# First product of the later slots of 256 rows in 7 products of half blocks, interleaved with the preceding slot's second product

## The chip, the cores and the metric

The kernel runs on one core of a Trainium2 chip. The metric is the device time of one execution in microseconds (us). The engines are PE (matrix products; PEld is its weight load), DVE, ACT and POOL (elementwise work) and SP (which issues most DMAs; "SPq" in a profile is its queue). DMAs move data between device memory and the on-chip memory (SBUF); products are accumulated in PSUM.

## What is computed

Two layers over 4096 tokens of width 256, all in float32. The second layer adds to each token a scan over time and the output of one of 8 experts, which is chosen by an argmax. This case is about the experts:

```
gate_logits = jnp.einsum('bsd,ed->bse', x, gate_w) + gate_b + expert_bias
top_idx = jnp.argmax(gate_logits, axis=-1)
for e in range(NUM_EXPERTS):                       # 8
    mask = (top_idx == e)[..., None].astype(x.dtype)
    h = jax.nn.relu(jnp.einsum('bsd,df->bsf', x, w1[e]) + b1[e])    # 256 -> 1024
    y = jnp.einsum('bsf,fd->bsd', h, w2[e]) + b2[e]                 # 1024 -> 256
    out = out + mask * y
```

The result is added to the token's row of the residual and the scan (the "base").

## The kernel before

The first layer and the scans come first (until about 900 us). By then the tokens lie in device memory sorted by expert (`xs_d`), each row with its token's number as a 257th column, and the base rows in `base_d`. Then come *slots*: 12 slots (`NF`) of 256 rows (`SL`, that is `SN` = 2 parts of 128), then slots of 128 rows, 8 (`MU`) always and further ones behind a test on the count `used`. A slot has one expert, read from `owner_i`; its rows begin at `at_i`.

For slot j:

- `weights(j)` (SP): four DMAs, w1 and w2 (1 MB each), b1 and b2, into tiles `w1p`, `w2p`, `b1p`, `b2p`. There are 3 of each for the slots of 256 rows and 3 others for those of 128.
- `slot_rows(j)` (SP): one DMA of the rows, from `xs_d` into `xrp` (4 tiles).
- `base_rows(j)` (POOL): an indirect DMA for each part, which gathers the base rows into `brp` (2 tiles) by the token numbers in `xrp`.
- `slot(j)` is a generator in five steps. Step 1: PE transposes the rows into `px` (L1104), and ACT (j < 2) or DVE copies them to `xTp` (L1106, L1108). Steps 2 and 3: the first product, 8 blocks f of 128 hidden units. For each, two matmuls (the two halves c of the 256 inputs) with 256 moving columns go to `ph` (L1114), and ACT (even f) or DVE (odd f) adds the bias, applies relu and writes `hT` (L1118, L1120); in slot 0 it is ACT alone. Step 4: the second product, for each of the two parts n 8 matmuls into `py` (L1127), and DVE adds the bias into `y` (L1130). Step 5: POOL adds the base rows (L1132) and scatters `y` to the output by indirect DMAs (L1134).

PE, SP, ACT and DVE run in the order in which the program is written; POOL's order in this stage is the scheduler's. The loop over the slots issues weights for slot j + 2 and rows for slot j + 2 at the start of slot j, then slot j's first product, the last step of slot j - 1, the transposes of slot j + 1, and slot j's second product. So on PE a slot is first product, transposes, second product. In slot 0, the transposes of slot 1 lie between the two products, and the last transposes of the scans (`pt`, L442), with the DVE adds (L445) and the write of `base_d` (L446) behind them, follow its second product.

The products of the first layer and the scan are already made of 7 products for 8 by `seven` (with Winograd's form of Strassen's scheme for 2x2 blocks); for the experts each block is multiplied as it is.

Of the kernel before, what the change touches and what calls it, by code (L numbers as in the profile page):

```python
# [47 lines left out]
PE, SP, ACT, DVE, POOL = (getattr(mybir.EngineType, k) for k in ("PE", "SP", "Activation", "DVE", "Pool"))  # L48
# [3 lines left out]
def tile_two_layers(  # L52
# [19 lines left out]
    nc = tc.nc  # L72
# [9 lines left out]
    ident = const.tile([P, P], F32, name="ident")  # L82
# [110 lines left out]
    psc1 = ctx.enter_context(tc.tile_pool(name="ps_scan", bufs=1, space=bass.MemoryType.PSUM))  # L193
# [231 lines left out]
    finished = []  # L425
# [47 lines left out]
    def rest_of(it):  # L473
        for _ in it:
            pass
# [9 lines left out]
    with ExitStack() as l0:  # L485
        wp = l0.enter_context(tc.tile_pool(name="w0", bufs=1, side="right"))
        wk = l0.enter_context(tc.tile_pool(name="work0", bufs=1, side="right"))
# [129 lines left out]
        def norm0(b, out):  # L617
            xn = wk.tile([P, NT, D], F32, name=f"xn_{b}", tag="xn")
            mv = small.tile([P, NT, 2], F32, name="mv")
            rstd = small.tile([P, NT], F32, name="rstd")  # L620
            out[b] = xnT = wk.tile([P, DC, TB], F32, name=f"xnT_{b}", tag="xnT", bufs=2)
            yield from layernorm(xs[b], xn, mv, rstd)
            yield
            if b == 0:

                fold()
                decay_mask()
                pt = [ps.tile([P, TB], F32, name=f"pt_{c}", tag=next(third)) for c in range(DC)]
# [12 lines left out]
            if b:  # L641
                cols0[b] = column_sums(wk, xnT, f"sums_{b}", 1)
            yield
# [249 lines left out]
        first = l0.enter_context(ExitStack())  # L893
# [4 lines left out]
        for b in range(NB):  # L898
            cols = cols0.pop(b)
            selb0 = selection(b, 0)  # L900
            back = norm1(b - 1) if b > 0 else iter(())
# [13 lines left out]
            if b + 1 < NB:  # L915
                ahead = norm0(b + 1, xnT)
# [25 lines left out]
        back = norm1(NB - 1)  # L942
# [24 lines left out]
    wk = ctx.enter_context(tc.tile_pool(name="work1", bufs=1, side="right"))  # L967
# [88 lines left out]
    sets = {}  # L1056
# [39 lines left out]
    def slot(j):  # L1096

        w1s, w2s, b1s, b2s = w1p(j), w2p(j), b1p(j), b2p(j)
        sn = parts(j)
        xr, xT, br = xrp(j), xTp(j)[:, :, : sn * P], brp(j)[:, :sn, :]  # L1100
        px = ps.tile([P, DC, sn * P], F32, name=f"px_{j}", tag="ps")
        for c in range(DC):
            for n in range(sn):
                nc.tensor.transpose(px[:, c, n * P : (n + 1) * P], xr[:, n, c * P : (c + 1) * P], ident)  # L1104
        if j < 2:
            nc.scalar.copy(xT, px)  # L1106
        else:
            nc.vector.tensor_copy(xT, px)  # L1108
        yield
        hT = wk.tile([P, FC, sn * P], F32, name=f"hT_{j}", tag="hT", bufs=2)  # L1110
        for f in range(FC):
            ph = ps.tile([P, sn * P], F32, name=f"ph_{j}_{f}", tag="ps")
            for c in range(DC):
                nc.tensor.matmul(  # L1114
                    ph, w1s[:, c, f * P : (f + 1) * P], xT[:, c, :], start=(c == 0), stop=(c == DC - 1)
                )
            if f % 2 == 0 or j == 0:
                nc.scalar.activation(hT[:, f, :], ph, AF.Relu, bias=b1s[:, f : f + 1])  # L1118
            else:
                nc.vector.tensor_scalar(hT[:, f, :], ph, b1s[:, f : f + 1], 0.0, ALU.add, ALU.max)  # L1120
            if f % (FC // 2) == FC // 2 - 1:
                yield
        y = wk.tile([P, sn, D], F32, name=f"y_{j}", tag="y", bufs=3)
        for n in range(sn):
            py = ps.tile([P, D], F32, name=f"py_{j}_{n}", tag="ps")
            for f in range(FC):
                nc.tensor.matmul(  # L1127
                    py, hT[:, f, n * P : (n + 1) * P], w2s[:, f, :], start=(f == 0), stop=(f == FC - 1)
                )
            nc.vector.tensor_add(y[:, n, :], py, b2s)  # L1130
        yield
        nc.gpsimd.tensor_add(y, y, br)  # L1132
        for n in range(sn):
            to = nc.gpsimd.indirect_dma_start(  # L1134
                out=out, out_offset=token(j, n), in_=y[:, n, :], in_offset=None, bounds_check=T - 1, oob_is_err=False
            )
            apart(to, written, "tokens' rows differ")
        yield


    scan_step(NB * UNITS - steps_done - 3 * CHUNKS + 1)
# [1 line left out]
    next(ends_filled)  # L1143
    scan_step(CHUNKS)
    rest_of(ends_filled)
    for j in range(3):
# [6 lines left out]
    cur, behind = slot(0), None  # L1153
    next(cur)
    used = nc.values_load(used_i[0:1, 0:1], min_val=MU, max_val=NU)

    taken = ExitStack()
    for j in range(NS):
        if j >= NF + MU:
            taken.enter_context(tc.If(used > j - NF))  # L1160
        if j + 2 < NS:
            weights(j + 2)
            if j > 0:
                slot_rows(j + 2)
        next(cur)
        next(cur)
        if behind:
            rest_of(behind)
        if j == 0:
            ahead = slot(j + 1)  # L1170
            next(ahead)
            next(cur)
            rest_of(finished.pop(0))
            base_rows(0)
# [4 lines left out]
            places(  # L1179
                tl, w1p=([P, DC, FF], 3), w2p=([P, FC, D], 3), b1p=([P, FC], 3), b2p=([P, D], 3),  # L1180
                xrp=([P, 1, D + 1], 4), xTp=([P, DC, P], 2), brp=([P, 1, D], 2),
            )
        if j + 1 < NS:
            base_rows(j + 1)
            if j > 0:
                ahead = slot(j + 1)
                next(ahead)
        if j > 0:
            next(cur)
        behind = cur  # L1190
        if j + 1 >= NF + MU:
            rest_of(behind)
            behind = None
        cur = ahead
    taken.close()


# [49 lines left out]
```

## Time and profile before

| | us |
|---|---|
| median of 3 runs | 1170.42 (1169.88 to 1173.16) |
| the profiled execution | 1170.57 |
| its span in the profile | 1168.8 |
| PE busy, share of the span | 1153.0, 99% |
| granted TensorE clock, mean | 0.998 |
| slots of 256 rows, first products start to slots of 128 rows | 902.27 to 1074.22 |
| slots of 128 rows, to the last second product's bias | 1074.22 to 1161.26 |

By stage, the busy times of the engines are:

| window, us | PE | PEld | DVE | ACT | POOL | DMA share |
|---|---|---|---|---|---|---|
| 931.9 to 1074.2 (slots 2 to 11) | 142.30 | 125.45 | 34.00 | 18.93 | 57.04 | 0.64 |
| 1074.2 to 1161.2 (slots of 128 rows) | 86.96 | 81.69 | 25.89 | 17.62 | 32.98 | 0.93 |

A line of the groups or of the timeline reads: line of the kernel, engine, operation, output<-inputs, shapes, count; then, in the groups, the busy time and the mean of one in ns, and the idle time before them with what ended it. In the timeline the first two columns are start and duration in us. In the chain of waits each line is a start, a duration and what ran then. A matmul of float32 stands as two instructions.

### The profile page before, as it was taken

The page shows a single profiled execution, that of the slowest core. Times are in us where ns is not written, and L with a number is a line of the kernel's source. Part 1 is how long each engine was busy: PE and PEld are TensorE (multiplying, and loading weights), DVE is VectorE, ACT ScalarE, POOL GpSimd, SP SyncE. Part 2 cuts the span into 40 slices and gives each one's busy share as a digit, 9 for nine tenths or more (in the row PEclk, how much of TensorE's full clock was granted, in tenths as well). Part 3 has the DMA queues.
Part 4 walks back from the last instruction along what each step waited for, and adds up shares of the span by engine and source line. Part 5 has one row for each costly group of instructions (what it writes and reads, how often), then busy time and mean ns, then how long its engine had stood idle before and what let it go on. Part 6 is the DMA issues. An engine that isn't in the chain of part 4 may idle for free.

```text
span 1168.8 us, 17270 instructions
## 1 busy us (share of the span) xinstructions
PE 1153.0 (99%) x6234; PEld 975.2 (83%) x6234; DVE 712.2 (61%) x1512; ACT 363.3 (31%) x719; POOL 314.6 (27%) x378
## 2 busy tenths in 40 slices
PE   8999999999999999999999999999999999999997
PEld 6887888888888888888888888888644888888996
DVE  5545736697579657876775797578799322222222
ACT  3112142444343333433343344343434111111221
POOL 6182220231014020402130231011053253333333
PEclk9999999999999999999999999999999999999999
DMA  8696563475256435535654465244258676683997
GB/s 255 214 352 236 156 218 144 141 240 186 99 185 212 146 139 167 201 135 178 223 192 135 148 203 186 100 167 154 90 155 250 246 236 214 212 300 134 332 367 265
DMA packets 89865, 231.33 MB, mean 198 GB/s; under 512 B 13885, under 2 KB 42705, under 8 KB 83121
## 3 DMA queue, kind: packets, MB, share of 16 engines
q1 hardware_dynamic: 81552, 202.77, 51.2%
q0 software_dynamic: 7792, 26.91, 6.3%
q8 instruction: 50, 0.82, 0.3%
q10 hardware_dynamic: 432, 0.52, 0.1%
q14 instruction: 39, 0.31, 0.1%
HBM read 206.75 MB, written 27.09 MB: 200 GB/s over the span
## 4 chain that ended last, share of the span: by engine, by line
PE 89%; DVE 5%; issue 2%; DMA 1%; POOL 1%; SPq 1%; ACT 0%; POOLq 0%; DVEq 0%
PE acc L765 21%; PE px_s L229 12%; PE px L229 10%; PE ph L1114 10%; PE py L1127 9%; PE pv_s L229 6%; PE pv L229 5%; PE py_s L229 3%; PE py L229 2%; PE px_yg L229 2%; PE pv L665 2%; PE po L711 1%; PE pv_yg L229 1%; PE pt L173 1%; DVE z L346 1%
## 5 line engine op out<-in xcount | busy, mean ns | idle before, releaser
L765 PE MATMUL acc<-vals,rs 128*128 128x256 f32 x1024 | 242.2, 380 | 0.0
L765 PEld LDWEIGHTS acc<-vals,rs 128*128 128x128 f32 x1024 | 194.2, 190 | 27.3 <-issue 1.4
L1114 PE MATMUL ph<-xTp,w1p 128*128 128x256 f32 (+1 forms) x768 | 129.8, 327 | 0.9 <-ACT xTp L1106 0.9
L1127 PE MATMUL py<-w2p,hT 128*128 128x256 f32 x576 | 128.3, 379 | 0.0
L1114 PEld LDWEIGHTS ph<-xTp,w1p 128*128 128x128 f32 x768 | 117.7, 191 | 11.4 <-ACT xTp L1106 1.1
L1127 PEld LDWEIGHTS py<-w2p,hT 128*128 128x128 f32 x576 | 107.7, 190 | 13.5
L348 POOL COPY last<-z 128x1 f32<-128x1 f32 x56 | 19.6, 352 | 340.6 <-DVE z L346 340.6
L1118 ACT ACTIVATE hT<-ph,b1p 128x256 f32<-128x256 f32 (+1 forms) x100 | 42.2, 422 | 212.4 <-PE ph L1114 157.6
L306 ACT ACTIVATE z<-z,bs 128x256 f32<-128x256 f32 (+1 forms) x156 | 87.4, 611 | 1.8 <-DVE z L255 1.8
L1120 DVE TENSOR_SCALAR hT<-ph,b1p 128x128 f32<-128x128 f32 (+1 forms) x92 | 38.1, 414 | 79.5 <-PE ph L1114 74.1
L229 PE MATMUL px_s<-sums,ws 128*128 128x256 f32 x312 | 81.3, 383 | 0.0
L1130 DVE TENSOR_TENSOR y<-py,b2p 128x256 f32<-128x256 f32 x36 | 15.3, 424 | 106.9 <-PE py L1127 94.9
L229 PE MATMUL px_s<-xn1T,ws 128*128 128x256 f32 x312 | 80.1, 379 | 0.0
L229 PE MATMUL pv_s<-sums,ws 128*128 128x256 f32 x312 | 80.1, 379 | 0.0
L346 DVE TENSOR_TENSOR_SCAN z<-z,last,z 128x512 f32<-128x512 f32 x56 | 75.7, 1351 | 0.0
L743 DVE SCALAR_TENSOR_TENSOR rs<-rs,selb 128x512 f32<-128x512 f32 x64 | 69.4, 1084 | 1.1
L229 PE MATMUL px<-xnT,keys 128*128 128x256 f32 x256 | 69.2, 393 | 0.1
L229 PE MATMUL px<-sums,keys 128*128 128x256 f32 x256 | 66.6, 383 | 0.0
L229 PE MATMUL pv<-sums,keys 128*128 128x256 f32 x256 | 66.5, 382 | 0.0
L229 PEld LDWEIGHTS px_s<-xn1T,ws 128*128 128x128 f32 x312 | 59.3, 190 | 8.1 <-issue 0.2
L229 PEld LDWEIGHTS pv_s<-sums,ws 128*128 128x128 f32 x312 | 59.3, 190 | 8.0
L229 PEld LDWEIGHTS px_s<-sums,ws 128*128 128x128 f32 x312 | 57.3, 190 | 9.9 <-ACT u_s L245 3.3
(236 smaller groups left out, 1842.3 us busy)
## 6 DMA issues: line engine op xcount, KB each, us to landing
ws<-wsum_d SPq DMA_DIRECT2D x39, 896.0 KB, 4.7
selb<-sel_d SPq DMA_DIRECT2D x64, 512.0 KB, 6.3
w1p<-in_w_dram SPq DMA_DIRECT2D x26, 1024.0 KB, 7.5
w2p<-in_w_dram SPq DMA_DIRECT2D x26, 1024.0 KB, 7.5
keys<-ksum_d SPq DMA_DIRECT2D x28, 896.0 KB, 8.6
vals<-in_e_vals_dram SPq DMA_DIRECT2D x32, 512.0 KB, 4.7
cb<-comb_d SPq DMA_DIRECT2D x32, 256.0 KB, 8.7
wsum_d<-wst POOLq DMA_DIRECT2D x6, 896.0 KB, 8.9
```

The costliest lines, as they stand in the source:

```text
L229: nc.tensor.matmul(to[:, q, :], w[:, q, at, :], cols[k - 1], start=start and q == 0, stop=True, skip_group_check=True,)
L306: nc.scalar.activation(z[ec][:, q, lo:hi], src[:, q, :], AF.Tanh if i == 1 else AF.Sigmoid, bias=bs[:, i, m, ec : ec + 1])
L346: nc.vector.tensor_tensor_scan(h, a[ec][:, m % 2, :], h, 0.0 if b == 0 else state, ALU.mult, ALU.add)
L348: nc.gpsimd.tensor_copy(state, h[:, TB - 1 : TB])
L665: nc.tensor.matmul(pv[-1][:, n % 2, :], xnT[:, c, n * P : (n + 1) * P], wv[:, c, :], start=(c == 0), stop=(c == DC - 1),)
L743: nc.vector.scalar_tensor_tensor(r[i][:, :, lo:hi], src, 0.0, selb[i][:, :, lo:hi], ALU.max, ALU.mult)
L765: nc.tensor.matmul(acc[n // 2][:, n % 2, :], lhsT, rhs, start=first and n % 2 == 0, stop=stop, skip_group_check=True)
L1114: nc.tensor.matmul(ph, w1s[:, c, f * P : (f + 1) * P], xT[:, c, :], start=(c == 0), stop=(c == DC - 1))
L1118: nc.scalar.activation(hT[:, f, :], ph, AF.Relu, bias=b1s[:, f : f + 1])
L1120: nc.vector.tensor_scalar(hT[:, f, :], ph, b1s[:, f : f + 1], 0.0, ALU.add, ALU.max)
L1127: nc.tensor.matmul(py, hT[:, f, n * P : (n + 1) * P], w2s[:, f, :], start=(f == 0), stop=(f == FC - 1))
L1130: nc.vector.tensor_add(y[:, n, :], py, b2s)
```

## The change

The slots of 256 rows are written as separate steps, and these are interleaved. While slot j's second product runs, the first product of slot j + 1 is made beside it: four times, a part of the first product and then a quarter of the second product (4 matmuls). After the second quarter come the transposes of slot j + 2. Slot 0's first product runs alone, and the transposes of slot 1 follow it.

For slots 4 to 11 (`PLAIN` = 4) the first product is made in 7 products (`first_sums7`). The blocks are: inner, the two halves c of the 256 inputs; rows of the result, hidden blocks of even and odd number (i); columns, the two parts k of 128 rows. One product is 4 matmuls (q) of 128 columns; three PSUM banks (`px`, `py`, `pv`) collect the products. The sums of weight blocks (4 of 128x512) are made by POOL one slot ahead, one of them in place in `w1p` (`first_weights`). The sums of row blocks (4 of 128x128) are made by DVE. DVE adds the bias and combines the banks (7 operations of 128x512), and ACT applies relu in place (4 of 128x512). The first products of slots 1 to 3, and of the slots of 128 rows, stay as they were.

The six tiles of each weight kind serve in turn (`in_turn`), for all slots, and weights are loaded three slots ahead. Rows of the slots of 256 are loaded for slots 0 to 3 ahead of all and then, behind slot j's scatter in the program, for slot j + 3. POOL's order in the slots is now the written one: in slot j the gathers of slot j + 1, the weight sums of slot j + 2, and slot j's last step. The slots of 128 rows keep their order of first product, transposes and second product.

```diff
-    w1p, w2p, b1p, b2p, xrp, xTp, brp = (placed(k) for k in ("w1p", "w2p", "b1p", "b2p", "xrp", "xTp", "brp"))
+    def in_turn(name):
+        return lambda j: [t for kind in sets[name] for t in kind][j % 6]
+    xrp, xTp, brp = (placed(k) for k in ("xrp", "xTp", "brp"))
+    w1p, w2p, b1p, b2p = (in_turn(k) for k in ("w1p", "w2p", "b1p", "b2p"))
...
+    PLAIN = 4
+    FP = FC // 2
+    wsums = {}
+    def quarters1(j):
+        w = w1p(j).rearrange("p c (q i h) -> p c q i h", q=FP, i=2)
+        return [w[:, c, :, i, :] for i in range(2) for c in range(DC)]
+    def first_weights(j):
+        a11, a12, a21, a22 = quarters1(j)
+        wsums[j] = tl.tile([P, 3, FP, P], F32, name=f"wsum1_{j}", tag="wsum1", bufs=2)
+        s4, s2, s3 = (wsums[j][:, k] for k in range(3))
+        nc.gpsimd.tensor_sub(s3, a11, a21)
+        nc.gpsimd.tensor_add(a21, a21, a22)
+        nc.gpsimd.tensor_sub(s2, a21, a11)
+        nc.gpsimd.tensor_sub(s4, a12, s2)
+    def first_sums7(j):
...
+        nc.vector.tensor_sub(t[:, 0, :], b12, b11)
+        nc.vector.tensor_sub(t[:, 1, :], b22, t[:, 0, :])
+        nc.vector.tensor_sub(t[:, 2, :], b22, b12)
+        nc.vector.tensor_sub(t[:, 3, :], b21, t[:, 1, :])
+        terms = {
+            1: (a11, b11), 2: (a12, b21), 3: (s4, b22), 4: (a22, t[:, 3, :]), 5: (s1, t[:, 0, :]),
+            6: (s2, t[:, 1, :]), 7: (s3, t[:, 2, :]),
+        }
+        def product(k, to, start):
+            w, x = terms[k]
+            for q in range(FP):
+                nc.tensor.matmul(
+                    to[:, q, :], w[:, q, :], x, start=start and q == 0, stop=True, skip_group_check=True
+                )
...
+        def biased(k, i, src):
+            u = tl.tile([P, FP, P], F32, name=f"ub{k}_{j}", tag=f"ub{k}")
+            nc.vector.tensor_tensor(u, src, bias[:, i].broadcast_to([P, FP, P]), ALU.add)
+            return u
+        def relu(i, k):
+            nc.scalar.activation(h[:, :, i, k, :], h[:, :, i, k, :], AF.Relu)
+        product(1, px, True)
+        product(2, py, True)
+        u1 = biased(1, 0, px)
+        nc.vector.tensor_add(h[:, :, 0, 0, :], py, u1)
+        relu(0, 0)
+        yield
+        product(6, px, False)
+        pv = psc1.tile([P, FP, P], F32, name=f"pv1_{j}", tag="pv")
+        product(7, pv, True)
+        u2 = biased(2, 1, px)
+        yield
+        product(5, px, False)
+        u4 = biased(4, 1, px)
+        nc.vector.tensor_add(h[:, :, 1, 1, :], pv, u4)
+        relu(1, 1)
+        yield
+        product(3, px, False)
+        product(4, pv, False)
+        nc.vector.tensor_add(h[:, :, 1, 0, :], pv, u2)
+        relu(1, 0)
+        nc.vector.tensor_tensor(h[:, :, 0, 1, :], px, bias[:, 0].broadcast_to([P, FP, P]), ALU.add)
+        relu(0, 1)
+        yield
...
+    ctx.enter_context(tc.manual_schedule(engines={POOL}))
+    rows(0)
     used = nc.values_load(used_i[0:1, 0:1], min_val=MU, max_val=NU)
+    rest_of(first(0, 4))
+    rows(1)
+    for j in range(NF):
+        weights(j + 3 if j else 2)
+        if j > 0:
+            base_rows(j + 1)
+            if PLAIN <= j + 2 < NF:
+                first_weights(j + 2)
+        if j + 1 < PLAIN:
+            ahead = first(j + 1, 4)
+        elif j + 1 < NF:
+            ahead = first_sums7(j + 1)
+        else:
+            ahead = first(j + 1, 2)
+        back = second(j)
+        for k in range(4):
+            next(ahead, None)
+            next(back)
+            if j == 0 and k == 0:
+                rest_of(finished.pop(0))
+                base_rows(0)
+                base_rows(1)
+            if k == 1:
+                rows(j + 2)
         if j == 0:
             table_only.close()
             scan_only.close()
...
+            weights(3)
+        finish(j)
+        if j > 0:
+            slot_rows(j + 3)
```

`rows`, `first`, `second` and `finish` are the old steps 1, 2 and 3, 4 and 5, with `second` giving way after each 4 matmuls.

More of the change, by code (lines that the diff above doesn't have):

```diff
@@ L1094, in base_rows, with rows @@
             nc.gpsimd.indirect_dma_start(out=brp(j)[:, n, :], out_offset=None, in_=base_d, in_offset=token(j, n))
-    def slot(j):
-        w1s, w2s, b1s, b2s = w1p(j), w2p(j), b1p(j), b2p(j)
+    hT, y = {}, {}
+    def rows(j):
         sn = parts(j)
-        xr, xT, br = xrp(j), xTp(j)[:, :, : sn * P], brp(j)[:, :sn, :]
+        xT = xTp(j)[:, :, : sn * P]
         px = ps.tile([P, DC, sn * P], F32, name=f"px_{j}", tag="ps")
@@ L1103, in slot @@
             for n in range(sn):
[L1104 removed]
+                nc.tensor.transpose(px[:, c, n * P : (n + 1) * P], xrp(j)[:, n, c * P : (c + 1) * P], ident)
         if j < 2:
@@ L1108, in slot, with hidden, first @@
             nc.vector.tensor_copy(xT, px)
-        yield
-        hT = wk.tile([P, FC, sn * P], F32, name=f"hT_{j}", tag="hT", bufs=2)
+    def hidden(j):
+        hT[j] = wk.tile([P, FC, parts(j) * P], F32, name=f"hT_{j}", tag="hT", bufs=2)
+        return hT[j]
+    def first(j, steps):
+        w1s, b1s = w1p(j), b1p(j)
+        sn = parts(j)
+        h = hidden(j)
         for f in range(FC):
@@ L1114, in slot @@
                 nc.tensor.matmul(
-                    ph, w1s[:, c, f * P : (f + 1) * P], xT[:, c, :], start=(c == 0), stop=(c == DC - 1)
+                    ph, w1s[:, c, f * P : (f + 1) * P], xTp(j)[:, c, : sn * P], start=(c == 0), stop=(c == DC - 1)
                 )
             if f % 2 == 0 or j == 0:
-                nc.scalar.activation(hT[:, f, :], ph, AF.Relu, bias=b1s[:, f : f + 1])
+                nc.scalar.activation(h[:, f, :], ph, AF.Relu, bias=b1s[:, f : f + 1])
             else:
-                nc.vector.tensor_scalar(hT[:, f, :], ph, b1s[:, f : f + 1], 0.0, ALU.add, ALU.max)
@@ L1121, in slot @@
-            if f % (FC // 2) == FC // 2 - 1:
+                nc.vector.tensor_scalar(h[:, f, :], ph, b1s[:, f : f + 1], 0.0, ALU.add, ALU.max)
+            if (f + 1) % (FC // steps) == 0:
                 yield
-        y = wk.tile([P, sn, D], F32, name=f"y_{j}", tag="y", bufs=3)
+    PLAIN = 4
[12 more added lines that the diff above has]
+        nc.gpsimd.tensor_sub(s4, a12, s2)
@@ new lines, in first_sums7 @@
+    def first_sums7(j):
+        a11, a12, s1, a22 = quarters1(j)
+        s4, s2, s3 = (wsums[j][:, k] for k in range(3))
+        b11, b12, b21, b22 = (xTp(j)[:, c, h * P : (h + 1) * P] for c in range(DC) for h in range(SN))
+        t = tl.tile([P, 4, P], F32, name=f"tsum1_{j}", tag="tsum1", bufs=2)
+        nc.vector.tensor_sub(t[:, 0, :], b12, b11)
[12 more added lines that the diff above has]
+                )
+        h = hidden(j).rearrange("p (q i) (k t) -> p q i k t", i=2, k=SN)
+        bias = b1p(j).rearrange("p (q i) -> p i q", i=2).unsqueeze(3)
+        def biased(k, i, src):
[4 more added lines that the diff above has]
+            nc.scalar.activation(h[:, :, i, k, :], h[:, :, i, k, :], AF.Relu)
+        px, py = (psc1.tile([P, FP, P], F32, name=f"p{k}1_{j}", tag=f"p{k}") for k in "xy")
+        product(1, px, True)
[21 more added lines that the diff above has]
+        yield
@@ L1124, in slot, with second @@
+    def second(j):
+        w2s, b2s = w2p(j), b2p(j)
+        sn = parts(j)
+        y[j] = wk.tile([P, sn, D], F32, name=f"y_{j}", tag="y", bufs=3)
         for n in range(sn):
@@ L1127, in slot, with finish @@
                 nc.tensor.matmul(
-                    py, hT[:, f, n * P : (n + 1) * P], w2s[:, f, :], start=(f == 0), stop=(f == FC - 1)
+                    py, hT[j][:, f, n * P : (n + 1) * P], w2s[:, f, :], start=(f == 0), stop=(f == FC - 1)
                 )
-            nc.vector.tensor_add(y[:, n, :], py, b2s)
-        yield
-        nc.gpsimd.tensor_add(y, y, br)
+                if f == FC // 2 - 1:
+                    yield
+            nc.vector.tensor_add(y[j][:, n, :], py, b2s)
+            yield
+    def finish(j):
+        sn = parts(j)
+        out_rows = y.pop(j)
+        nc.gpsimd.tensor_add(out_rows, out_rows, brp(j)[:, :sn, :])
         for n in range(sn):
             to = nc.gpsimd.indirect_dma_start(
-                out=out, out_offset=token(j, n), in_=y[:, n, :], in_offset=None, bounds_check=T - 1, oob_is_err=False
+                out=out, out_offset=token(j, n), in_=out_rows[:, n, :], in_offset=None, bounds_check=T - 1,
+                oob_is_err=False,
             )
             apart(to, written, "tokens' rows differ")
-        yield
     scan_step(NB * UNITS - steps_done - 3 * CHUNKS + 1)
@@ L1145, in tile_two_layers @@
     rest_of(ends_filled)
-    for j in range(3):
+    for j in range(4):
         slot_rows(j)
@@ L1152, in tile_two_layers @@
         pieces.pop(0)()
-    cur, behind = slot(0), None
-    next(cur)
+    ctx.enter_context(tc.manual_schedule(engines={POOL}))
+    rows(0)
     used = nc.values_load(used_i[0:1, 0:1], min_val=MU, max_val=NU)
[L1157 to L1168, printed above, removed]
-        if j == 0:
[L1170 to L1174, printed above, removed]
+    rest_of(first(0, 4))
[22 more added lines that the diff above has]
+                rows(j + 2)
+        if j == 0:
             table_only.close()
@@ L1182, in tile_two_layers @@
             )
+            weights(3)
+        finish(j)
+        if j > 0:
+            slot_rows(j + 3)
+    taken = ExitStack()
+    behind = None
+    for j in range(NF, NS):
+        if j >= NF + MU:
+            taken.enter_context(tc.If(used > j - NF))
+        if j + 3 < NS:
+            weights(j + 3)
+        if NF < j < NS - 2:
+            slot_rows(j + 2)
+        if j > NF:
+            rest_of(first(j, 2))
+        if behind:
+            finish(behind)
         if j + 1 < NS:
             base_rows(j + 1)
[L1185 to L1190, printed above, removed]
+            if j > NF:
+                rows(j + 1)
+        rest_of(second(j))
+        behind = j
         if j + 1 >= NF + MU:
-            rest_of(behind)
+            finish(behind)
             behind = None
-        cur = ahead
     taken.close()
```

## The prediction

> **What bounds the kernel now.** I read the page's busy times and slices first, then the costliest groups, then the chain of waits, then the timeline of single slots.
>
> ```profile
> PE 1153.0 (99%) x6234; PEld 975.2 (83%) x6234; DVE 712.2 (61%) x1512; ACT 363.3 (31%) x719; POOL 314.6 (27%) x378
> ...
> PEclk9999999999999999999999999999999999999999
> ...
> L1114 PE MATMUL ph<-xTp,w1p 128*128 128x256 f32 (+1 forms) x768 | 129.8, 327 | 0.9 <-ACT xTp L1106 0.9
> L1127 PE MATMUL py<-w2p,hT 128*128 128x256 f32 x576 | 128.3, 379 | 0.0
> ```
>
> PE is busy 99% at the full granted clock, and the two products of the slots (L1114, L1127) waited 0.9 us in all. The next lines, from the chain of waits late in the slots of 256 rows and at the start of those of 128, give the price of a matmul in both widths:
>
> ```profile
> 1053.28 6.91 PE py L1127 x32
> 1060.19 6.91 PE ph L1114 x32
> 1067.09 0.22 PE px L1104 x2
> 1067.31 6.91 PE py L1127 x32
> 1074.22 3.57 PE ph L1114 x32
> 1077.79 0.22 PE px L1104 x2
> 1078.01 3.46 PE py L1127 x16
> ```
>
> 32 instructions of 256 columns take 6.91 us (0.216 each), 32 of 128 columns 3.57 (0.1116 each, not half of 0.216). A slot of 256 rows is 6.91 + 0.44 (transposes) + 6.91 = 14.25 us without a hole. So in this stage a matmul taken away is time gained, if no wait takes its place.
>
> **The change, part by part.**
>
> *Removed.* Slots 4 to 11 have their first product in 7 products of 4 matmuls of 128 columns; each matmul is two instructions (16 matmuls stand as 32 rows above). 56 x 0.1116 = 6.25 us instead of 6.91: 0.66 a slot, 8 x 0.66 = 5.3 us. Were 128 columns at half of 256 (0.108), it would be 6.05 and 6.9 us in all. I take 5.3, as the tail's row is the very shape.
>
> *Moved: slot 0.* The first product of slot 1 now follows that of slot 0 directly, before slot 0's second product. Its rows must have been copied first (ACT, behind eight activations of slot 0):
>
> ```profile
> 909.48 0.47 ACT L1118 ACTIVATE hT<-ph,b1p 128x256 f32<-128x256 f32 x1 [0.39 <-PE ph L1114]
> 909.71 7.07 PE L1127 MATMUL py<-w2p,hT 128*128 128x256 f32 x32
> 909.91 0.58 ACT L1106 COPY xTp<-px 128x512 f32<-128x512 f32 x1
> ```
>
> Before, py starts at 909.71 and hides the copy, which ends at 910.49. After, PE starts at 910.49 + 0.06 (the step from this copy's end at 902.21 to PE at 902.27 in slot 0) = 910.55: 0.84 us lost, once. Everything later on PE is behind it.
>
> *Added: work on DVE, ACT and POOL in slots 3 to 10, beside PE.* I lay a new slot of 13.60 us out from its start: products 1, 2 to 1.79, a quarter of the second product (1.73) to 3.51, products 6, 7 to 5.30, quarter to 7.03, transposes to 7.46, product 5 to 8.35, quarter to 10.08, products 3, 4 to 11.87, quarter to 13.60. DVE's row for PSUM + SBUF, 128x512, is 0.69 (L239), one following another after 0.60 (two of L445 take 1.28). A reader of PSUM starts about 0.25 after PE goes on.
> - Product 3 needs the copy u4 of product 5: 8.35 + 0.25 + 0.69 = 9.29, before 10.08. Product 4 needs the sum behind it, 9.89, before 10.98.
> - The next slot's product 1 needs the last two sums out of px: 11.87 + 0.25 + 0.60 + 0.69 + 0.06 = 13.47, before 13.60. That is the tightest cover, 0.13. If each sum were 0.1 longer, it would cost 0.07 a slot; I take nothing.
> - ACT has four activations (0.72 each by L306's 128x512) where it had four of 0.47; the last is done by 11.87 + 0.25 + 0.60 + 0.69 + 1.4 = 14.8, and the second product reads its rows at 13.6 + 7.5. Nothing.
> - Product 6 needs u1, and u1 stands on DVE behind the last y add of the slot before (0.25 to 0.67) and four sums of 128x128 with two SBUF inputs (0.29 each by L993, some 0.3 apart). Free of POOL, u1 is done near 2.6 against 3.51. But POOL starts its own y add (1.26) 0.09 after DVE's:
>
> ```profile
> 377.24 0.72 POOL L217 TENSOR_TENSOR sums<-xnT 128x256 f32<-128x256 f32 x1
> 377.54 0.68 DVE L255 TENSOR_TENSOR rs<-pv,u 128x512 f32<-128x512 f32 x1
> 378.26 1.48 DVE L743 SCALAR_TENSOR_TENSOR rs<-rs,selb 128x1024 f32<-128x1024 f32 x1
> 378.62 1.71 POOL L218 TENSOR_TENSOR sums<-xnT,sums 128x256 f32<-128x256 f32 x1
> 379.67 1.21 DVE L355 TENSOR_TENSOR z<-z,cb 128x512 f32<-128x512 f32 x1
> ```
>
> These lines say who is slowed: beside POOL, DVE's op out of PSUM keeps its 0.68, ops with two SBUF inputs stretch (0.69 alone, 1.21 here), and POOL's too (0.72 to 1.71). So the seven big DVE ops are safe from POOL's new sums, but the four small ones can lose up to 1.26 to POOL's y add, once a slot. Then u1 ends at 2.6 + 1.2 = 3.8 in the worst case: 0 to 0.3 a slot, 0 to 2.4 in all. With the dead time of the blocked sum partly absorbed (901.81 to 903.59 for an op of 0.69 whose blocker ended at 903.03: 0.56 after), 3.5 to 3.6: I take 0.08 a slot, 0.6.
>
> The Trainium skill ("SBUF — State Buffer", Who interferes with whom) has the rule behind these rows: VectorE and GpSimd share one pair of ports by an exclusive lock, and a VectorE op with two SBUF inputs is shut out for the whole of a GpSimd op that reads SBUF. It speaks against the four sums beside POOL's y add: by it a full 1.26 is lost in each slot, u1 ends at 3.8, and the sum below would hold 2.4 where I put 0.6.
>
> - POOL starts 0.76 into a slot (behind DVE's y add), needs 1.26 + 0.28 for its y add and 5.2 for four indirect DMAs some 1.3 apart, which is 7.5; then come the four new sums of 128x512, 1.26 each by the y add, done at 12.5 of 13.6, the third at 11.3. They serve the next slot, whose product 6 is the first to read one (the third), at 13.6 + 3.5 = 17.1: cover 5.8. Bounds of one sum: 1.26 (alone) and 2.6 (xn1T sums of L219 take 1.51 against 0.72 alone, 2.1 times). I take 1.26, as only DVE's four small sums read SBUF twice here. Nothing.
>
> *Moved: loads.* Weights come three slots ahead into six buffers, four DMAs a slot on SP, no longer held by the buffer of two slots ago. The fourth rows load goes before slot 1's weights on SP (1.2 us a load from 892.95 to 894.15): w1p then is issued at 897.7, lands 5.12 later by its row, 902.8, and is needed at 910.55. Slot 3's weights wait on SP for the transposes of the last scan (about 915), needed near 940. One more set of weights (27, not 26) is loaded at the end for nobody; the last output's DMA (1162.76) ends the kernel as before. In the tail SP asks for the same bytes per 7.25 us. All at nothing.
>
> *A new wait of slot 4's rows.* Their load on SP waits until slot 0's output is scattered, and slot 0's output waits on POOL behind the write of base_d and the two gathers. Before, gathers began 6.9 after base_d was issued (919.67 to 926.55). Now base_d is out near 916.9, but beside 4.4 MB of weights: 7 to 13, then gathers 5.2, y add and scatter 4, landing 4.6, rows 4.1: 941.8 to 947.8; PE asks at 946.8. Queued behind that load are slot 5's weights, wanted 15 us later. Bounds 0 and 1 (3 with the slowest rows load, 6.3). I take 0.
>
> *Sum.* -5.3 + 0.84 + 0.6 = -3.9 us. The profiled execution took 1170.57 (span 1168.8 and 1.8 around it); minus 3.9 it is 1166.7, and the median of before, 0.15 lower, gives 1166.6, 0.33% under 1170.42. I count as no change what lies within 0.3%, 3.5 us, so this is close to that edge.
>
> **Rivals.**
> - *The gain is half eaten, no measurable change.* POOL's lock every slot (2.4) and slot 4's rows (1): -5.3 + 0.84 + 3.4 = -1.1, 1169.3. For it: the lock's rows. Against: u1 needs nearly the whole 1.26 to be late.
> - *POOL becomes the bound, slower.* The place is product 6's wait for the weight sums. With c for one sum, POOL needs 6.74 + 4c a slot; above c = 1.7 that is more than 13.6, and it falls behind by the difference, six times over the eight slots. The third sum is then ready at 7.5 + 3c plus this, against 17.1. The gain of 3.9 is used up near c = 2.03 (7.5 + 6.1 + 6 x 1.26 - 17.1 = 4.1). At 2.2 it loses 7.5 + 6.6 + 11.6 - 17.1 = 8.6, which makes 1175.1; at 2.6, 7.5 + 7.8 + 21.2 - 17.1 = 19.4 and 1186. For it: L218 above. Against: what stretched those were DVE ops with two SBUF inputs, four short ones a slot here.
> - *Two widths cost nothing extra*, 0.108 an instruction, no lock: -6.9 + 0.84 = -6.1, 1164.3.
> - *It does not do what it says.* Not here: the built order shows 28 matmuls of 128 columns a slot in slots 4 to 11, alternating with quarters of the second product.
>
> **Numbers.** Forecast (1165.8 to 1168.0) 0.55, of which 0.38 are beyond 0.3%; half eaten 0.18; POOL-bound or another wait that costs more than the gain 0.17; cheaper matmuls 0.10. Faster 0.48, within 0.3% 0.34 (0.17 of the forecast, 0.17 of the eaten), slower 0.18. The range goes from 1164.4 to 1172.0.
>
> **What would show it.** The first product's 56 instructions at 0.1116 and a slot pitch of 13.6 to 13.7 in slots 4 to 10; an idle PE of 0.8 before the first product of slot 1, put down to ACT's copy; a hole before product 6 of 0 to 0.3, put down to DVE; POOL's sums at 1.26. I am wrong if the pitch stays at 14.2 or above, if PE waits for POOL at product 6 or 3, or if slot 2 has a hole before its transposes.

## The result and the profile after

| | before | after |
|---|---|---|
| median, us | 1170.45 (6 runs, 1169.37 to 1173.16) | 1166.17 (6 runs, 1165.61 to 1167.15) |
| ratio, 95% interval | | 0.9964 [0.9954, 0.9973] |
| profiled execution, us | 1170.57 | 1166.05 |
| its span | 1168.8 | 1164.3 |
| slot 0's first product on PE starts | 902.27 | 902.37 |
| last output's scatter on POOL starts | 1162.76 | 1158.58 |
| between the two ("the stage") | 260.49 | 256.21 |

The change saves 4.3 us, 0.36%, where 3.9 were forecast. Of the 4.5 us by which the span fell, 4.28 lie in the stage of the slots; 0.1 is lost ahead of it and 0.3 won behind the last scatter. PE's work ahead of the stage is the same in all kernels here, and yet its end moves between 900.86 and 905.64 from one execution to the next. So below, stages are compared, each from one profiled execution, and the medians beside them. (How well a stage repeats is seen in two variants below, e6 and e8, which agree with the changed kernel to 0.01. That the medians also differ by just 4.28 is chance: the six runs of before spread over 3.8 us and those of after over 1.5.)

The page of the changed kernel, the lines that answer to those of before (busy times, the slices' clock, and two groups):

```profile
PE 1147.5 (99%) x6426; PEld 976.8 (84%) x6426; DVE 750.1 (64%) x1568; ACT 368.1 (32%) x719; POOL 356.5 (31%) x410
...
PEclk9999999999999999999999999999999999999999
...
L1223 PE MATMUL py<-w2p,hT 128*128 128x256 f32 x576 | 133.9, 380 | 0.0
...
L1129 PE MATMUL ph<-xTp,w1p 128*128 128x128 f32 (+1 forms) x512 | 75.0, 302 | 1.5 <-ACT xTp L1113 1.5
```

PE has 5.5 us less to do and is as full as before. The first products that stayed plain (L1129) now wait 1.5 instead of 0.9 us, and for ACT: once at the start of the stage, as before, and once more in slot 0. PE has no other wait in the stage.

The chain of waits of this profile breaks off at its last entry, so the slots are read from the timeline. PE's lines in one slot of the new form (start, duration, engine, line, operation, count; a duration's end is modelled and runs into the next start):

```profile
1007.06 1.89 PE L1223 MATMUL py<-w2p,hT 128*128 128x256 f32 x8
1008.79 1.05 PE L1175 MATMUL px<-xTp,w1p 128*128 128x128 f32 x8
1009.68 1.06 PE L1175 MATMUL py<-xTp,w1p 128*128 128x128 f32 x8
1010.58 1.89 PE L1223 MATMUL py<-w2p,hT 128*128 128x256 f32 x8
1012.31 1.05 PE L1175 MATMUL px<-tsum,wsum 128*128 128x128 f32 x8
1013.20 1.06 PE L1175 MATMUL pv<-tsum,wsum 128*128 128x128 f32 x8
1014.09 1.89 PE L1223 MATMUL py<-w2p,hT 128*128 128x256 f32 x8
1015.82 0.60 PE L1111 MATMUL px<-ident,xrp 128*128 128x128 f32 x4
```

Products 1 and 2 start at 1008.79 and end where the quarter starts, at 1010.58: 16 instructions in 1.79, 0.112 each. Product 6 starts at 1012.31, 1.73 after that quarter, so without a hole. From transposes to transposes (1002.22, 1015.82) a slot takes 13.60, where it took 14.25.

DVE's lines around the start of the same slot:

```profile
1007.87 0.68 DVE L1211 TENSOR_TENSOR hT<-px,b1p 128x512 f32<-128x512 f32 x1
1009.00 0.42 DVE L1228 TENSOR_TENSOR y<-py,b2p 128x256 f32<-128x256 f32 x1 [0.44 <-PE py L1223]
1009.34 0.28 DVE L1163 TENSOR_TENSOR tsum<-xTp 128x128 f32<-128x128 f32 x1
1009.65 1.27 DVE L1164 TENSOR_TENSOR tsum<-xTp,tsum 128x128 f32<-128x128 f32 x1
1010.84 0.28 DVE L1165 TENSOR_TENSOR tsum<-xTp 128x128 f32<-128x128 f32 x1
1011.04 0.33 DVE L1166 TENSOR_TENSOR tsum<-xTp,tsum 128x128 f32<-128x128 f32 x1
1011.30 0.68 DVE L1184 TENSOR_TENSOR ub<-px,b1p 128x512 f32<-128x512 f32 x1
```

and POOL's two at the same time, the fourth weight sum and the y add:

```profile
1006.41 1.27 POOL L1155 TENSOR_TENSOR wsum<-w1p,wsum 128x512 f32<-128x512 f32 x1
1009.50 1.27 POOL L1235 TENSOR_TENSOR y<-y,brp 128x512 f32<-128x512 f32 x1 [1.82 <-DVE y L1228]
```

The second row sum (L1164) takes 1.27 where its neighbours of the same shape take 0.28 to 0.33. It ends 0.15 after POOL's y add (1010.92 against 1010.77), so it runs as if shut out for as long as that add lasts. But u1 (L1184), which product 6 waits for, still ends at 1011.98, 0.33 before product 6 starts. Not all of the 0.33 is spare: where PE does wait for u1, in e5 below, it goes on 0.14 after u1's end, which leaves some 0.19. The other tight cover is the last sum out of `px` (L1211): it ends at 1008.55, 0.24 before the next product 1. POOL's weight sums are 1.27 long and POOL waits 1.82 a slot for its y add.

The one new hole, in slot 0 (PE, around the transposes of slot 1's rows):

```profile
909.38 0.60 PE L1111 MATMUL px<-ident,xrp 128*128 128x128 f32 x4
910.66 2.00 PE L1129 MATMUL ph<-xTp,w1p 128*128 128x256 f32 x8 [0.68 <-ACT xTp L1113]
912.49 1.67 PE L1223 MATMUL py<-w2p,hT 128*128 128x256 f32 x7
```

The transposes end at about 909.82 (0.44 after their start) and PE goes on at 910.66, 0.84 later. The eight instructions after the stop take 1.83 (910.66 to 912.49) and not 1.73 as everywhere else.

### The profile page after: what moved, and what is told of

The parts are those of the page before. It is cut to its first block, busy times and chain, and to the rows that moved or that the text cites. A ratio compares the mean times of both kernels' runs of the same rounds, so it can differ in the third digit from the quotient of the medians.

```text
span 1164.3 us, 17738 instructions
## 1 busy us (share of the span) xinstructions
PE 1147.5 (99%) x6426; PEld 976.8 (84%) x6426; DVE 750.1 (64%) x1568; ACT 368.1 (32%) x719; POOL 356.5 (31%) x410
## 5 line engine op out<-in xcount | busy, mean ns | idle before, releaser
L1223 PE MATMUL py<-w2p,hT 128*128 128x256 f32 x576 | 133.9, 380 | 0.0
L1129 PE MATMUL ph<-xTp,w1p 128*128 128x128 f32 (+1 forms) x512 | 75.0, 302 | 1.5 <-ACT xTp L1113 1.5
L1129 PEld LDWEIGHTS ph<-xTp,w1p 128*128 128x128 f32 x512 | 68.8, 192 | 5.6 <-ACT xTp L1113 2.0
L322 PE MATMUL p<-xn1T,wr 128*128 128x512 f32 x144 | 63.4, 595 | 1.1 <-ACT z L325 1.1
L306 ACT ACTIVATE z<-px_s,bs 128x256 f32<-128x256 f32 x78 | 32.7, 470 | 99.1 <-PE px_s L229 99.1
L1133 ACT ACTIVATE hT<-ph,b1p 128x128 f32<-128x128 f32 (+1 forms) x68 | 27.1, 398 | 112.4 <-PE ph L1129 66.8
```

The costliest lines, as they stand in the source:

```text
L306: nc.scalar.activation(z[ec][:, q, lo:hi], src[:, q, :], AF.Tanh if i == 1 else AF.Sigmoid, bias=bs[:, i, m, ec : ec + 1])
L322: nc.tensor.matmul(p, w[:, q, 2 * ec + c, :], xn1T[b][:, c, :], start=(c == 0), stop=(c == DC - 1))
L1129: nc.tensor.matmul(ph, w1s[:, c, f * P : (f + 1) * P], xTp(j)[:, c, : sn * P], start=(c == 0), stop=(c == DC - 1))
L1133: nc.scalar.activation(h[:, f, :], ph, AF.Relu, bias=b1s[:, f : f + 1])
L1223: nc.tensor.matmul(py, hT[j][:, f, n * P : (n + 1) * P], w2s[:, f, :], start=(f == 0), stop=(f == FC - 1))
```

## The experiments

Theory: in the stage, the seven products give 0.65 for each slot that has them and nothing takes any of it back; the new order loses about 0.9 once, in slot 0; POOL has room. Rivals: the shut-out of DVE's row sums costs something in each slot; POOL's weight sums limit the slots; the widths of the matmuls, not their number, made the gain.

| kernel | stage, us | against after | median (runs) | ratio to before, 95% interval |
|---|---|---|---|---|
| before | 260.49 | +4.28 | | |
| after | 256.21 | | 1166.17 (6) | 0.9964 [0.9954, 0.9973] |
| e1, no slot in 7 products | 261.44 | +5.23 | 1171.79 (12) | 1.0014 [1.0002, 1.0026] |
| e2, slots 8 to 11 in 7 | 258.82 | +2.61 | 1169.26 (10) | 0.9984 [0.9974, 0.9993] |
| e3, slot 1's rows earlier | 255.27 | -0.94 | 1164.62 (6) | 0.9946 [0.9932, 0.9960] |
| e4, slots 4 to 11 in 8 of half width | 263.36 | +7.15 | 1174.20 (10) | 1.0024 [1.0014, 1.0033] |
| e5, e3 and slot 3 in 7 | 256.62 | +0.41 | 1166.15 (5) | 0.9963 [0.9949, 0.9977] |
| e6, 1 more weight sum on POOL | 256.21 | 0.00 | 1166.60 (4) | 0.9957 [0.9942, 0.9972] |
| e7, 4 more | 274.43 | +18.22 | 1184.64 (4) | 1.0124 [1.0108, 1.0139] |
| e8, row sums a slot earlier | 256.21 | 0.00 | 1166.36 (5) | 0.9958 [0.9945, 0.9971] |
| e9, e5 with POOL's sums moved | 254.62 | -1.59 | 1164.56 (5) | 0.9944 [0.9931, 0.9957] |
| e10, e9 and slot 2 in 7 | 253.97 | -2.24 | 1163.98 (6) | 0.9941 [0.9927, 0.9955] |

The medians of before in the three groups of runs (e1 to e4, e5 to e8, e9 and e10) were 1171.17, 1170.83 and 1171.11.

### e1 and e2: the new order alone, and half of the gain

```diff
-    PLAIN = 4
+    PLAIN = 12
```

In e2 the number is 8.

> The whole change but the 7 products: all twelve slots of 256 rows keep two matmuls of 256 columns for each hidden block, interleaved as in the changed kernel. Theory (a bound PE has fewer columns to multiply): the 5.3 us of the 7 products come back and the 0.84 us of slot 0 stays, so a median of about 1171.4 and a span of about 1169.6, and a pitch of 14.25 us in slots 4 to 10. Rival (the interleaving, the written POOL order and the earlier weights bring the gain, and the products are hidden anyway): about 1166.

> 7 products in slots 8 to 11 alone, 4 of the 8. Theory: half the gain, 2.65 us over the kernel with none, so a median of about 1168.8 and a span of about 1167.0. A gain that hangs on a start or an end (once, not by the slot) would lie at one of the ends, 1166 or 1171.

Taking the seven products away from all eight slots costs 5.23, from four of them 2.61: 0.65 a slot, and straight. So the gain goes by the slot, and it is what the removed instructions cost (6.91 less 56 at 0.112 is 0.64): the straight line alone would not exclude a loss in every slot, but the price leaves no room for one, and e8 tests it directly. Without the seven products the new order is 0.95 slower than before (261.44 against 260.49): the interleaving alone brings nothing and costs the hole of slot 0. The whole runs show this less clearly (the ratio is 1.0014 with an interval that just leaves out 1, the medians differ by 0.05%). Whether the seven products could be had without the interleaving was not tried.

### e3: slot 1's rows before the last quarter of slot 0's first product

```diff
-    rest_of(first(0, 4))
-    rows(1)
+    start = first(0, 4)
+    for _ in range(3):
+        next(start)
+    rows(1)
+    rest_of(start)
```

> The changed kernel, with slot 1's transposes and their copy put before the last two hidden blocks of slot 0's first product instead of behind them. Theory (PE waits 0.84 us there for ACT's copy): the wait goes and nothing takes its place, a span of 1163.5 and a median of about 1165.3. Rival (the wait only moves on to the next thing that ACT is late with): a span of 1164.3 as it is.

PE's lines of e3 at the place of the hole:

```profile
906.58 0.60 PE L1111 MATMUL px<-ident,xrp 128*128 128x128 f32 x4
907.02 3.62 PE L1129 MATMUL ph<-xTp,w1p 128*128 128x256 f32 x16
910.48 1.89 PE L1223 MATMUL py<-w2p,hT 128*128 128x256 f32 x8
```

The last quarter of slot 0's product and the first of slot 1's stand behind the transposes as 16 instructions in one piece (3.46, 0.216 each): the copy is hidden. The stage gives back 0.94, that is the stop of 0.84 and the 0.10 by which the eight instructions after it were longer. So the cost of the new order can be had back. That this version beats the changed kernel rests on the stages, which differ by 0.94; the intervals of the two ratios overlap at their ends.

### e4: the same blocks without the saved product

The first products of slots 4 to 11 in 8 products of half width, in the plain order of blocks:

```diff
-            for c in range(DC):
+            for n, c in [(n, c) for n in range(sn) for c in range(DC)] if 4 <= j < NF else []:
+                nc.tensor.matmul(
+                    ph[:, n * P : (n + 1) * P], w1s[:, c, f * P : (f + 1) * P], xTp(j)[:, c, n * P : (n + 1) * P],
...
-    PLAIN = 4
+    PLAIN = 12
```

> As the run with no 7 products, but slots 4 to 11 make their first product in 8 products of half blocks: 64 instructions of 128 columns instead of 32 of 256. Theory (128 columns cost 0.1116, more than half of 0.216): 64 x 0.1116 = 7.14 against 6.91, 0.23 a slot, 1.8 us over the run with no 7 products, a span of about 1171.4 and a median of 1173.2. Rival (the width costs nothing, 0.108): the same as that run, 1169.6 and 1171.4.

A quarter of the first product in e4 (PE; 16 instructions of 128 columns), and the quarter of the second product behind it:

```profile
1006.91 1.95 PE L1129 MATMUL ph<-xTp,w1p 128*128 128x128 f32 x16
1008.70 1.89 PE L1228 MATMUL py<-w2p,hT 128*128 128x256 f32 x8
```

16 instructions of 128 columns take 1.79 (1006.91 to 1008.70), eight of 256 take 1.73. Against e1 the stage is 1.92 longer, 0.24 a slot. So narrow matmuls cost a little, and the gain is due to their number: 64 at half width are 0.24 dearer than 32 whole ones, 56 are 0.65 cheaper. The rival of the cheaper matmuls, 0.108 each, falls. By the Trainium skill a product of true float32 is four passes through the array ("FP8 and Floating Point Precision", TensorE Precision Notes), and an isolated warm matmul of N columns takes N/2.4 + 2.5 ns ("TensorE: Matmul & The Clock Gate", Back-to-back issue gap). Worked out from these pages, an estimate for a float32 matmul is 223 ns at 128 columns and 437 at 256, so two halves are 10 ns dearer than a whole one; the rows here have 224 and 432, so 16 ns, or 0.26 over the 16 matmuls of a slot, where the stages give 0.24. For a stream with weight loads the same section of the page states about 81 ns at 128 columns; four times that, an estimate of 324 ns, is not what the rows show.

### e5: one more slot in 7 products, where there is POOL work in the way

e3, and

```diff
-    PLAIN = 4
+    PLAIN = 3
```

> The run with slot 1's transposes put early, and 7 products from slot 3 on, not slot 4: a ninth slot. Theory: 0.66 us less than that run in the stage of the slots (254.6 from slot 0's first product to the last scatter, where that run has 255.3), if POOL is done in time. In slot 1 of the changed kernel POOL is free at 939.4; the third of the new sums would be ready some 3.9 later, 943.3, and product 6 of slot 3 asks at 940.1 + 3.5 = 943.6: a cover of 0.3. Rival (POOL, still behind from the write of base_d, is late): a hole before product 6 in slot 2, put down to POOL, and no gain or a loss.

This missed: 256.62 instead of 254.6. PE's line at the start of product 6 of slot 3 in e5:

```profile
939.85 1.89 PE L1223 MATMUL py<-w2p,hT 128*128 128x256 f32 x8
943.51 1.13 PE L1175 MATMUL px<-tsum,wsum 128*128 128x128 f32 x8 [1.77 <-DVE ub L1184]
```

Product 6 was due at 941.58 and starts at 943.51, 1.93 late, for DVE's u1. DVE's lines before it:

```profile
938.61 1.34 DVE L1163 TENSOR_TENSOR tsum<-xTp 128x128 f32<-128x128 f32 x1
939.98 1.31 DVE L1164 TENSOR_TENSOR tsum<-xTp,tsum 128x128 f32<-128x128 f32 x1
941.22 0.28 DVE L1165 TENSOR_TENSOR tsum<-xTp 128x128 f32<-128x128 f32 x1
941.42 1.35 DVE L1166 TENSOR_TENSOR tsum<-xTp,tsum 128x128 f32<-128x128 f32 x1
942.69 0.68 DVE L1184 TENSOR_TENSOR ub<-px,b1p 128x512 f32<-128x512 f32 x1
```

and POOL's weight sums beside them:

```profile
938.53 1.27 POOL L1153 TENSOR_TENSOR w1p<-w1p 128x512 f32<-128x512 f32 x1
939.88 1.27 POOL L1154 TENSOR_TENSOR wsum<-w1p 128x512 f32<-128x512 f32 x1
941.23 1.39 POOL L1155 TENSOR_TENSOR wsum<-w1p,wsum 128x512 f32<-128x512 f32 x1
```

The sum that product 6 reads (L1154) is done at 941.15, in time, and my expectation had priced nothing else. But three of the four row sums were shut out, each by one of POOL's sums, and u1 ended at 943.37. So this run shows what the shut-out costs without cover: the 1.93, and 0.07 by which the 16 instructions after the stop were longer (943.51 to 945.37, 1.86 instead of 1.79). With the gain of a slot, 0.65, that is the +1.35 against e3.

### e6 and e7: more work on POOL

One more sum in each `first_weights`, into a tile that nothing reads; in e7 the loop runs four times:

```diff
         nc.gpsimd.tensor_sub(s4, a12, s2)
+        extra = tl.tile([P, FP, P], F32, name=f"extra_{j}", tag="extra")
+        for _ in range(1):
+            nc.gpsimd.tensor_sub(extra, a12, s2)
```

> The changed kernel with one more weight sum of 128x512 on POOL in each of slots 2 to 9 (its result is used by nothing). In the changed kernel POOL's last sum ends 12.5 us into a slot of 13.6 and its y add begins 0.7 into the next: cover 1.8. One more sum takes 1.36. Theory: no change, 256.2 us in the stage. Rival (POOL already sets the pace, or its longer work shuts DVE out at a place that PE waits for): some 1 us a slot longer.

> As before, with four more sums in each of these slots. POOL's work then ends 17.9 into a slot and its next y add would have begun at 14.3: it falls behind by 3.6 a slot, six times, 21.7, and the cover before product 6 reads its sum is 17.1 - 11.1 = 6.0. Theory (POOL becomes the bound as the slower rival of the prediction has it): about 15.7 us lost, 272 in the stage, with PE waiting for POOL at product 6. Rival (POOL's order leaves room elsewhere, or slot rows come late first): well below 8, or holes before the transposes and not before product 6.

One more sum goes into POOL's wait before its y add, which falls from 1.82 to 0.58 (in the same slot as above), and costs nothing. Four more cost 18.22. The waits of PE in e7 (in all, times, longest):

```profile
PE px L1178 <- POOL wsum L1154: 7.9, 3, 3.1
PE px L1178 <- DVE ub L1187: 5.6, 5, 2.0
```

So POOL can become the bound at the place that the prediction named, product 6, and by the shut-out of DVE as well: all eight slots stop there, three for the weight sum and five for u1. The changed kernel is away from that point by more than one sum a slot. The 2.5 us above what I had expected of e7 are no wait; they are in the section on the hardware.

### e8: the row sums out of POOL's way

```diff
+            if k == 3 and PLAIN <= j + 2 < NF:
+                row_sums(j + 2)
```

with the four row sums taken out of `first_sums7` into `row_sums`, so that DVE makes them before the y add and not beside it.

> The changed kernel with DVE's four row sums of the next slot put before, not behind, the last y add of a slot, where POOL has ended its sums and not yet begun its y add. Theory (the second row sum is shut out by POOL's y add for its whole length, but the cover before product 6 is 0.33 us longer than the loss): the second row sum falls from 1.26 to 0.3, and the stage stays at 256.2. Rival (that lock costs PE time in a place that I do not see): 0.3 us a slot, 2.4 less.

The second row sum in the changed kernel, all eight (durations in ns, least, median and most):

```profile
L1164 DVE TENSOR_TENSOR tsum<-xTp,tsum x8: 1258/1261/1266, 955.3 to 1050.4; 128x128 f32<-128x128 f32 x8
```

and in e8:

```profile
L1163 DVE TENSOR_TENSOR tsum<-xTp,tsum x8: 291/292/294, 953.0 to 1049.0; 128x128 f32<-128x128 f32 x8
```

The shut-out is gone, 0.97 us in each slot, and the stage is the same to 0.01. In the changed kernel it is there in each slot and costs nothing.

### e9 and e10: the weight sums where POOL waits

In the changed kernel POOL waits 9.35 us between the write of `base_d` (916.44) and the first gather (926.61). e9 is e5 with the sums of slot 3 there; for it the opening of the pools and `weights(3)` come up from the end of slot 0. e10 has slot 2 in 7 products as well (`PLAIN = 2`, and `first_weights(2)` ahead of `first_weights(3)`).

```diff
-    PLAIN = 4
+    PLAIN = 3
...
-            if PLAIN <= j + 2 < NF:
+            if 4 <= j + 2 < NF:
                 first_weights(j + 2)
...
             if j == 0 and k == 0:
                 rest_of(finished.pop(0))
+                table_only.close()
+                scan_only.close()
...
+                weights(3)
+                first_weights(3)
                 base_rows(0)
```

> Slot 1's transposes early, 7 products from slot 3 on, and the weight sums of slot 3 moved on POOL to where it waited 9.3 us in the changed kernel, between the write of base_d and the gathers that read it. Theory (in the run with 7 products from slot 3 on, POOL's sums ran beside DVE's row sums and shut them out; nothing else stood in the way): POOL has no sums to make when slot 2 begins, the hole of 1.8 before product 6 goes, and the stage is 0.66 shorter than with 7 products from slot 4 on, 254.6 for 255.3. Rival (the gathers, now behind the sums, are late for slot 0's output and slot 4's rows): a hole before the transposes of slot 2.

> The same with slot 2 as well: two sets of weight sums in POOL's wait. Theory: another 0.66, 253.9, if POOL is done with both sets before slot 1 begins at about 924.6. Its second set waits for slot 3's weights, which are issued at 915.4 and landed about 7 later, so it would run from 922.5 to 927.9 and shut out DVE's row sums of slot 1, three of them for up to 1.27 each: a hole of 1 to 2 before product 6 of slot 1, and 255 or more. If the weights land sooner, 253.9.

POOL in e9, from the first of these sums to the first gather:

```profile
919.13 1.26 POOL L1152 TENSOR_TENSOR wsum<-w1p 128x512 f32<-128x512 f32 x1 [4.32 <-DMA w1p<-in_w_dram]
920.48 1.26 POOL L1153 TENSOR_TENSOR w1p<-w1p 128x512 f32<-128x512 f32 x1
921.81 1.27 POOL L1154 TENSOR_TENSOR wsum<-w1p 128x512 f32<-128x512 f32 x1
923.16 1.27 POOL L1155 TENSOR_TENSOR wsum<-w1p,wsum 128x512 f32<-128x512 f32 x1
924.59 1.03 POOL L1100 DMA_INDIRECT brp<-base_d,xrp  x1 [0.15 <-issue]
```

The sums lie in the wait and the gathers start 10.6 after the write of `base_d` (913.98), where they did 10.2 after it. Product 6 of slot 3 then starts 1.73 after the quarter before it, without a stop, and e9 gains the 0.65 of its slot over e3; e10 gains the next 0.65. In e10 that came by neither of the two ways that I expected: POOL's second set ran from 921.95 to 927.26, past the start of the slot at 925.28, but it met only the second row sum of that slot (926.14, 1.27 long) and not three of them, and the cover before product 6 took that in as in the other slots. e10 is the best version found, 1163.98, under both kernels (0.9941 of before). That it is better than e9 and e3 rests on the stages, as the medians' intervals overlap.

## Why the prediction was right

- *The removed products, -5.3.* Measured 5.23 (e1 against after), in equal parts for each slot (e2). The price of 0.1116 from the tail's row held: 0.112 in the changed slots and in e4.
- *Slot 0, +0.84.* The stop was 0.84, and put down to ACT's copy; in all the new order lost 0.95 (e1 against before) and 0.94 came back in e3. What the step left out is 0.10 for slower instructions right after a stop.
- *The lock of DVE and POOL, +0.6.* This is the term that was mis-sized: it cost 0. The shut-out itself comes in each of the eight slots, 1.26 for a sum that takes 0.29 in e8, and that agrees with the rule of the Trainium skill ("SBUF — State Buffer", Who interferes with whom). It puts off the chain by 0.99 (1.19 from L1164 to L1165 instead of 0.20): about what I had reckoned (2.6 to between 3.5 and 3.6), and less than the 1.2 of my worst case. What was wrong is the chain that it is added to. Without the shut-out u1 would end 2.2 into the slot (3.19 measured, less 0.99) and not 2.6, because the small sums follow one another after 0.20 (1010.84 to 1011.04) and not after 0.3, and the y add of DVE starts at 0.21 and not at 0.25. So u1 is not at the edge of its cover of 3.51. Even a loss of the full 1.26 would have put u1 at about 3.5 and not at 3.8. e5 shows the same stretch three times over with no cover left: 1.93 in one slot.
- *Covers that were put at nothing.* The next slot's product 1 had 0.24 where 0.13 was worked out; product 6 had its weight sum 6.0 ahead (1006.32 against 1012.31), where 5.8 was worked out; POOL's sums were at 1.27. Slot 4's rows were asked for at 938.39, and PE's transposes of them at 947.05 had no wait. PE's only waits in the stage are for ACT's copy, once as before and once in slot 0.
- *The sum.* -5.23 + 0.95 = -4.28 in the stage, against -3.9. These two parts add up by construction, as both are taken against e1; what speaks for them independently is e2's half of the gain and e3's 0.94. The difference of 0.4 is the lock (-0.6), slot 0 (+0.1) and the products (+0.1).
- *The rivals.* "Half eaten" falls with e8 (no price of the lock) and with slot 4's rows. "POOL becomes the bound" has its mechanism confirmed by e7 and its condition refuted by e6 and the sums' 1.27. "Two widths cost nothing extra" falls with e4.

## What to carry to other kernels

A saved product is worth its instructions at the price of a row of the same width, and whether it is kept is seen by laying each added operation against the time at which PE asks for it, with every operation that can shut it out drawn in at full length. A shut-out that costs nothing in one slot can cost its whole length in another where its cover is gone, so when a loop's work is extended by one more turn, look at what stands beside it there, not only at when its own result is due. Added work belongs into a wait that the engine has anyway.

## What was not expected of the hardware

In e7, the longest stop of PE was followed by slow matmuls. Windows of e7 over the stop and what follows (start and end, length, busy time and instructions of PE, PEld, DVE, ACT and POOL, granted clock, DMA share, GB/s):

```profile
1034.20:1034.70 0.50, 0.00 (x0) 0.00 (x0) 0.00 (x0) 0.00 (x0) 0.42 (x2) 1.00 0.72 156
1034.70:1035.20 0.50, 0.00 (x0) 0.00 (x0) 0.00 (x0) 0.00 (x0) 0.50 (x1) 0.79 0.93 323
1035.20:1035.90 0.70, 0.00 (x0) 0.00 (x0) 0.00 (x0) 0.00 (x0) 0.70 (x1) 0.50 0.48 91
1039.50:1041.00 1.50, 1.50 (x6) 1.23 (x5) 0.00 (x0) 0.00 (x0) 1.42 (x2) 0.50 0.98 401
...
1041.50:1042.00 0.50, 0.50 (x3) 0.38 (x3) 0.00 (x0) 0.00 (x0) 0.50 (x1) 0.69 0.39 104
1042.00:1042.40 0.40, 0.40 (x4) 0.30 (x3) 0.00 (x0) 0.00 (x0) 0.40 (x1) 1.00 0.02 5
```

PE stood from 1032.66 (1030.93 and the quarter's 1.73) to 1035.95, 3.3 us. The clock fell to 0.50 in the middle of the window that shows 0.79, at about 1034.99 (half the clock for 0.42 of its time), and came back at about 1041.8 (half for 0.62 of the window with 0.69). Products 6 and 7 and the quarter took 6.44 (1035.95 to 1042.39) instead of 3.51, so this stop cost 2.93 more than its length. That is the excess of e7: without it the eight stops make 15.3, where 15.7 was expected. The next longest stops of e7, 2.5 us (1016.43 to 1018.95 is one), left the clock at 1.00. But a shorter stop than 3.3 can do the same. In the profiled execution of e6, far ahead of the stage, PE stood 2.69 us (87.87 to 90.56) and the clock was halved from 90.12 to 93.53; at the same place in the changed kernel it stood 2.66 us (87.93 to 90.59) at the full clock. PE's line after the stop of e6, the window of e6 with the halved clock (columns as above), and PE's line after the stop of the changed kernel:

```profile
90.56 2.08 PE L229 MATMUL px_yg<-sums,both 128*128 128x256 f32 x4 [2.53 <-POOL sums L218]
90.13:93.53 3.40, 2.97 (x7) 2.44 (x8) 3.19 (x7) 0.82 (x2) 3.24 (x6) 0.50 0.33 125
90.59 1.13 PE L229 MATMUL px_yg<-sums,both 128*128 128x256 f32 x4 [2.50 <-POOL sums L218]
```

So a stop is not priced by its length alone: 2.69 us halved the clock and 2.66 did not.

The Trainium skill ("TensorE: Matmul & The Clock Gate", What's actually happening) states that the clock is halved after an idle window of about 3.4 us, and given back after a busy one, by windows that run freely. These runs agree in the times: 1034.99 to 1041.8 are two such windows, 90.12 to 93.53 is one. Laid out in steps of 3.413 from a change of the clock in the same run, the windows also tell the stops apart. The two windows ahead of a halved clock hold 2.33 idle us (1032.66 to 1034.99) and 2.25 (87.87 to 90.12). The stops that left the clock alone are cut by the end of a window: the 2.52 of e7 at 1017.92 (five steps before 1034.99), the 2.66 of the changed kernel at 88.75 (314 steps before 1160.54, where its clock falls after the last matmuls). No window holds more than 1.84 idle us of them. A stop of 2.04 us in e6 (155.17 to 157.21) lies within one window and left the clock at 1.00. So a window need not be idle throughout, though the page's words ask for an idle window: 2.25 of 3.41 us were enough here, and 2.04 were not. This is worked out from five stops; no run moved a stop to try it.

After the short stops the clock is granted in full, and still the next instructions are slower: 0.10 in the first eight of 256 columns (in after and in e1, 1.83 instead of 1.73). Why is open.
